# A new table of pieces for a four-layer graph network: where the projections and the feed-forward parts stand between the attention steps

## The chip, the cores and the metric

The kernel runs on one core of one Trainium2 chip. The metric is the device time of one launch in microseconds (us); less is better. Four engines share the work: PE (TensorE, the matrix unit, with its weight loads shown apart as PEld), DVE (VectorE), ACT (ScalarE) and POOL (GpSimd). SP (SyncE) issues the transfers.

## The reference

The input is `x`, 16 graphs of 1024 nodes with 128 features, and one 1024 x 1024 adjacency matrix `adj`. Three transformer layers and one graph attention layer follow each other. Cut to what matters:

```python
# layers 0, 1, 2 (8 heads of 16)
Q, K, V = (h @ Wq), (h @ Wk), (h @ Wv)               # split into heads
scores = einsum('bnhd,bmhd->bhnm', Q, K) / sqrt(16)
attn = softmax(where(adj == 0, -inf, scores))
x = layer_norm(h + (attn @ V) @ Wo + bo)
x = layer_norm(x + relu(x @ W1 + b1) @ W2 + b2)
# layer 3
h = x @ W
e = leaky_relu(h @ a_src [:, None] + h @ a_dst [None, :])
out = layer_norm(softmax(where(adj == 0, -inf, e)) @ h + x)
```

## The kernel before

**Blocks, halves and steps.** One graph in one of the layers 0 to 2 is a block; there are 48. Four graphs go through the three layers side by side, so the order is layer 0 of graphs 0 to 3, layer 1 of graphs 0 to 3, layer 2 of graphs 0 to 3, then the same for the next four graphs. A block has four halves: two groups of four heads (`g`) times two halves of the queries (`qh`). A half has eight steps, one for each 128 keys (`kt` 0 to 7). A block thus has 32 steps, and "step 12" below means the step at position 12 of its block.

**What a step issues.** `score_step` computes the scores of four heads for 128 keys and 512 queries: four matmuls (L423) into two PSUM tiles `s` of 1024 columns. For three of the eight `kt` (2, 5, 7, `BOTH_ON_DVE`) DVE adds the mask to both tiles (L433). For the others, ACT takes the exponential of the first tile straight from PSUM (L430) and POOL multiplies the mask in (L431), while DVE adds the mask to the second tile. Whatever DVE has masked gets its exponential on ACT afterwards (L445). Then `av_due` issues the attention product of the step four earlier (`AHEAD = 4`): matmuls (L450) into the accumulator `acc`. After the eighth product of a half, `finish` lets DVE transpose the accumulator into `tt` (L461), and only then may the first product of the next half write `acc`, since there is one such tile (`sums`). With a lag of four steps, the last product of a half is issued in steps 3, 11, 19 and 27, and the first product of the next half in steps 4, 12, 20 and 28.

**Buffers in PSUM.** There are three tiles `s` of two banks each, one bank `t` for all pieces (`bank()`), and the one accumulator. The scores of step n use two of the three tiles: the first needs the second tile of step n-2 to be read, the second needs the first tile of step n-1 to be read.

**Pieces.** Everything else is cut into pieces, and `piece()` issues at most one of them in a step, behind the product. A block's pieces are:

- `proj_tasks`, for the next block: `t0(0)`, `t0(1)` transpose the halves of `x` (L286, evicted by ACT); `split("Wk", h)` and `split("Wq", h)` project k and q (below K0, K1, Q0, Q1). ACT copies the bank into `hi` (L385), then DVE subtracts `hi` from the bank into `lo` (L386), and the bank is free only after both. `v(h)` projects v (ACT copies).
- `post_tasks`, for the block before: `both` (two DVE transposes L477, nothing on PE), `out_proj(h)` (op0, op1: DVE adds the residual, L329, and takes statistics, L322 and L324; then POOL normalises, L337 to L341), `x1t(h)` (transposes of the normalised rows, ACT evicts), `ffn1(f, h)` (f00, f10, f01, f11 by f and h; ACT applies the relu, L506), `ffn2(h)` (F20, F21: twice as many matmuls, and the same DVE and POOL work as `out_proj`).
- `last_tasks`, for the fourth layer of a graph that has left layer 2: two transposes, three pieces of node projections (`nodes`), `rows_gh` with 16 small DMAs, edges (L610 on DVE) and aggregations of 124 to 128 matmuls, and an end with POOL work and the output DMA.

**Order.** The engines PE and ACT keep the order in which this code issues; DVE, POOL and SP are ordered by the scheduler. The table `AT` gives each piece of `proj` and `post` the earliest step of its block; a chain's pieces stay in order. `last_tasks` have gaps instead of steps, stand in the same chain behind the `post` pieces of their block, and take any step whose piece isn't due. `piece()` asks the chains in order, `proj` first. By reading the queues, the pieces of a block without `last_tasks` fall like this (30 of the 48 blocks):

```
step    0   3    6    8   9  10   11 12  14 17 19 20 22  23   25   26  27  28  30
before  F20 t0.0 t0.1 F21 K0 both K1 op0 Q0 Q1 v0 v1 op1 x1t0 x1t1 f00 f10 f01 f11
```

In the 12 blocks with `last_tasks` throughout, almost every other step is taken too. `stack` (L408) brings `hi` and `lo` into the layout of the scores with 16 DMAs on SP; it is issued for the next block's first group at step 21, after its last projection.

Of the kernel before, what the change touches and what calls it, by code (L numbers as in the profile page):

```python
# [30 lines left out]
FIRST = 1  # L31


AT = {"proj": (3, 6, 9, 11, 14, 17, 19, 20), "post": (12, 22, 23, 25, 26, 27, 28, 30, 32, 40, 41)}
AT_END = {3: (12, 21, 22, 24, 25, 26, 27, 28, 30, 31), 2: (8, 9, 13, 14, 15, 16, 17, 18, 20, 21)}
AHEAD = 4
BOTH_ON_DVE = (2, 5, 7)
TILES = {"w": 10, "x": LANES + 1, "last": 2}
# [77 lines left out]
def fast_path(ctx: ExitStack, tc: tile.TileContext, a: dict, out: bass.AP, flag):  # L116
# [160 lines left out]
    def soon():  # L277

        return nullcontext() if head[0] else tc.high_priority(offset=SOON)
# [22 lines left out]
    def rows(v, n=NT):  # L302
        return v[:, None, :].to_broadcast([P, n, D])
# [53 lines left out]
    def proj_tasks(m):  # L357
        b, l = blocks[m]
        w = W[l]
        s = {}  # L360

        def t0(h):
            def run():
                x = state["x", b]
                if l == 0:
                    s["xT", h] = transpose_half("xT", x, h)
                    if h == 1:
                        nc.gpsimd.tensor_add(x, x, rows(w["bo"]))
                else:

                    s["xT", h] = transpose_half("xT", x, h, W[l - 1]["ln2_gc"], W[l - 1]["ln2_bc"])
                    if h == 1:
                        scale_shift(x, W[l - 1]["ln2_g"], w["bo"])
            return run

        def split(n, h):
            def run():
                if h == 0:
                    state[n, m] = [work.tile([P, N], F32R, tag="hl", name=i, bufs=4) for i in ("hi", "lo")]
                hi, lo = state[n, m]  # L380
                c = slice(h * 512, (h + 1) * 512)
                ps = bank()
                by_columns(ps, w[n], s["xT", h])
                with soon():
                    nc.scalar.copy(hi[:, c], ps)  # L385
                    nc.vector.tensor_sub(lo[:, c], ps, hi[:, c].bitcast(F32))  # L386
            return run

        def v(h):
            def out(ts, ps):  # L390
                with soon():
                    nc.scalar.copy(v_bufs[m % 2][:, ts].rearrange("p t h s -> p (t h) s")[:, :, :HD],
                                   ps.rearrange("p (m d) -> p m d", d=HD))
            return lambda: project([s["xT", h]], [w["Wv"]], h, out)

        pieces = [t0(0), t0(1), split("Wk", 0), split("Wk", 1), split("Wq", 0), split("Wq", 1), v(0), v(1)]
        return [(2 if n in (3, 4, 5, 6) else 1, f, {0: "+w", 1: "+w", 6: "-w", 7: "-w"}.get(n, "")) for n, f in enumerate(pieces)]

    behind = {}

# [68 lines left out]
    def post_tasks(b, l):  # L469
        w = W[l]  # L470
        s = {}
        att, recs = state["A"], state["recs"]

        def gather(h):
            def run():
                s["aT", h] = half_tile("aT")
                nc.vector.transpose(s["aT", h], att[:, h].rearrange("p k g d -> p (k g d)"))  # L477
                if h == 1:
                    check_range(recs.rearrange("p g h k -> p (g h k)"))
            return run  # L480

        def out_proj(h):
            def run():
                if h == 0:
                    s["n1"] = with_stats(state["x", b])
                project([s["aT", h]], [w["Wo"]], h, add_and_stats(s["n1"]))
                normalise(s["n1"], slice(4 * h, 4 * h + 4))
            return run

        def x1t(h, alone=False):  # L490
            def run():
                x1 = s["n1"][0]
                s["x1T", h] = transpose_half("x1T", x1, h, w["ln1_gc"], w["ln1_bc"])
                if alone:
                    scale_shift(x1[:, 4 * h:4 * h + 4, :], w["ln1_g"], w["b2"])
                elif h == 1:
                    scale_shift(x1, w["ln1_g"], w["b2"])
            return run

        def ffn1(f, h):  # L500
            def run():
                s["h", f, h] = half_tile("hT")
                ps = bank()
                by_columns(ps, w["W1"][:, f * P:(f + 1) * P], s["x1T", h])
                with soon():
                    nc.scalar.activation(s["h", f, h], ps, AF.Relu, bias=w["b1"][:, f:f + 1], scale=1.0)  # L506
            return run

        def ffn2(h):
            def run():  # L510
                if h == 0:
                    s["n2"] = with_stats(state["x", b])
                project([s["h", f, h] for f in range(NF)], [w["W2"][:, f, :] for f in range(NF)], h,
                        add_and_stats(s["n2"]))
                normalise(s["n2"], slice(4 * h, 4 * h + 4))
            return run

        def both():
            gather(0)()
            gather(1)()  # L520


        together = [(5, both, "+w +w"), (1, out_proj(0), "-w"), (1, out_proj(1), "-w"), (5, x1t(0), "+w"), (1, x1t(1), "+w")]
        for h in range(2):
            together += [(1, ffn1(0, h), "+w"), (1, ffn1(1, h), "+w -w")]
        together += [(1, ffn2(0), "-w -w"), (1, ffn2(1), "-w -w")]
        alone = [[(1, gather(h), "+w"), (1, out_proj(h), "-w"), (3, x1t(h, True), "+w"), (1, ffn1(0, h), "+w"),
                  (1, ffn1(1, h), "+w -w"), (1, ffn2(h), "-w -w")] for h in range(2)]
        return together, alone
# [161 lines left out]
    def piece():  # L691
        for chain in chains:
            if is_due(chain) and take(chain):
                return
# [27 lines left out]
    waiting = deque()  # L722
# [39 lines left out]
    n = 0  # L762
    with tc.manual_schedule(engines={mybir.EngineType.PE, mybir.EngineType.Activation}):
        for m, (b, l) in enumerate(blocks):
            order = [(g, qh) for g in range(G) for qh in range(2)]
            if m in (0, len(blocks) - 1):
                order.sort(key=lambda x: x[1])
            for at, (g, qh, kt) in enumerate((g, qh, kt) for g, qh in order for kt in range(NT)):
                now[0] = n
                if at == (6 if m == 0 else 1):  # L770
                    stack(m, 1)
                if n == 6:
                    with tc.issue_after(behind["stack"]):
                        first_weights()
                        other_weights()
                if n == 20:
                    with tc.issue_after(behind["pool"]):
                        biases()
                if n == 40:
                    with tc.issue_after(behind["dve"]):  # L780
                        last_weights()
                if at == 0 and m + 2 < len(blocks) and blocks[m + 2][1] == 0:
                    put([(0, fetch(blocks[m + 2][0]), "+x")], ("fetch", blocks[m + 2][0]))
                if m + 1 < len(blocks):
                    if at == (6 if m == 0 else 0):
                        need(("post",) + (blocks[m + 1][0], blocks[m + 1][1] - 1) if blocks[m + 1][1] else
                             ("fetch", blocks[m + 1][0]))
                        put(proj_tasks(m + 1), ("proj", m + 1), first=True)
                    if at == (24 if m == 0 else 21):
                        need(("proj", m + 1))  # L790
                        stack(m + 1, 0)
                step = m, g, qh, kt
                if FIRST <= n < FIRST + 4:

                    with tc.manual_schedule(engines={mybir.EngineType.DVE}):
                        e = score_step(step)
                        neighbours(4 + n - FIRST)
                        masks(4 + n - FIRST, mask_rows(4 + n - FIRST))
                else:
                    e = score_step(step)  # L800
                waiting.append((step, e, n + AHEAD))
                av_due(n)
                piece()
                n += 1
        exponentials(0)
        for n in range(n, n + 2 * AHEAD):
            now[0] = n
            av_due(n)
            piece()
        tail[0] = True  # L810
        while chains:
            now[0] += 1
            for chain in list(chains):
                if is_due(chain):
                    take(chain)
# [11 lines left out]
    both = const.tile([1, 2], F32)  # L827
# [224 lines left out]
```

## Time and profile before

| | |
|---|---|
| median of 3 runs | 3983.76 us (3979.37 to 3984.21) |
| the profiled execution | 3983.09 us, of which the span is 3981.2 us |
| granted TensorE clock | 0.987 |
| busy in the span | PE 3758.5, DVE 3408.3, ACT 3392.8, POOL 3331.4 us |
| a block without `last_tasks` (from 1440.72) | 73.14 us; busy PE 70.67, ACT 69.26, DVE 65.12, POOL 64.62 us |
| a block with them (from 931.92) | 97.01 us |

The time of a block is the distance between the first score matmuls of two blocks in the timeline of PE; a step's likewise. A matmul's end in the trace is modelled, and matmuls overlap, so the work of PE is read here from the distances between starts. PE counts as busy in nearly all of the span for that reason, whether or not it is at its peak.

### The profile page before, as it was taken

To read this page: it belongs to the slowest core of one execution; us is meant where nothing else is said; L and a number is where in the kernel's file an instruction comes from. 1 tells how busy PE (TensorE), PEld (TensorE's weight loads), DVE (VectorE), ACT (ScalarE), POOL (GpSimd) and SP (SyncE) were. 2 spreads that over 40 slices of the span, in tenths; PEclk is the share of its full clock that TensorE was granted. 3 is DMA by queue.
4 is the path that set the end of the run, shared out by engine and by line. 5 is a ranking of instruction groups with operands and counts; after the bars stand their busy time and mean duration, and the time that the engine had idled before them with its cause. 6 is when DMAs were issued, how large, how long until landed. Compare 5 with 4: busy or idle time off the path is not lost.

```text
span 3981.2 us, 107823 instructions
## 1 busy us (share of the span) xinstructions
PE 3758.5 (94%) x44501; PEld 1558.5 (39%) x44501; DVE 3408.3 (86%) x5326; ACT 3392.8 (85%) x3961; POOL 3331.4 (84%) x3010
## 2 busy tenths in 40 slices
PE   7999999999999999999999999999999999999996
PEld 2333333344443333334444333333444433333345
DVE  7888988988888988988888898888888898898874
ACT  7999999977779999997777999999777799999860
POOL 4788888987789888988778888888877898898875
PEclk8999999999999999999999999999999999999998
DMA  6222222112222222222222222221222212222200
GB/s 163 65 65 53 55 65 63 46 48 65 56 58 57 65 65 54 54 65 55 55 55 55 65 53 56 65 64 45 55 55 55 71 46 62 65 51 58 66 8 20
DMA packets 124465, 233.13 MB, mean 59 GB/s; under 512 B 34624, under 2 KB 73792, under 8 KB 123968
## 3 DMA queue, kind: packets, MB, share of 16 engines
q1 hardware_dynamic: 123056, 225.74, 22.5%
q8 instruction: 354, 5.80, 0.6%
q14 instruction: 143, 1.17, 0.1%
q10 hardware_dynamic: 912, 0.42, 0.0%
HBM read 15.54 MB, written 8.39 MB: 6 GB/s over the span
## 4 chain that ended last, share of the span: by engine, by line
PE 61%; DVE 22%; POOL 9%; ACT 4%; issue 3%; SPq 0%; DMA 0%; DVEq 0%; ACTq 0%; POOLq 0%
PE acc L450 23%; PE t L297 19%; PE s L423 16%; DVE e L433 13%; POOL e L431 3%; POOL x L341 2%; PE t L286 2%; DVE lo L386 2%; DVE st L322 2%; ACT e L445 2%; ACT e L430 2%; DVE tt L461 1%; POOL mv L339 1%; PE s L297 1%; POOL x L345 1%
## 5 line engine op out<-in xcount | busy, mean ns | idle before, releaser
L433 DVE TENSOR_TENSOR e<-s,mask_add 128x1024 f32<-128x1024 f32 x2112 | 2493.6, 1213 | 344.6 <-PE s L423 263.7
L445 ACT ACTIVATE e<-e 128x1024 f32<-128x1024 f32 x2112 | 2203.4, 1060 | 206.1 <-DVE e L433 187.9
L431 POOL TENSOR_TENSOR e<-e,mask 128x1024 f32<-128x1024 f32 x960 | 1933.5, 2026 | 419.0 <-ACT e L430 419.0
L450 PE MATMUL acc<-e,v 128*17 128x512 f32 x12288 | 1627.8, 601 | 73.3 <-DVE tt L461 47.8
L423 PE MATMUL s<-Wq,Wk 64*128 64x512 f32 x6144 | 1185.0, 456 | 58.1 <-DVE e L433 41.3
L430 ACT ACTIVATE e<-s 128x1024 f32<-128x1024 f32 x960 | 980.8, 1022 | 227.5 <-PE s L423 226.5
L423 PEld LDWEIGHTS s<-Wq,Wk 64*128 64x128 f32 x6144 | 501.2, 185 | 1027.9 <-DVE e L433 417.1
L450 PEld LDWEIGHTS acc<-e,v 128*17 128x17 f32 x12288 | 208.6, 95 | 582.1 <-issue 452.0
L341 POOL TENSOR_SCALAR x<-x,mv 128x128 f32<-128x128 f32 x896 | 389.1, 447 | 23.5
L345 POOL TENSOR_TENSOR x<-x,ln_g 128x1024 f32<-128x1024 f32 (+1 forms) x97 | 229.5, 2367 | 25.1 <-PE t L286 22.6
L339 POOL TENSOR_TENSOR mv<-mv,half_neg 128x4 f32<-128x4 f32 x224 | 232.4, 1038 | 18.6
L297 PE MATMUL t<-hd,e 128*32 128x129 f32 x7040 | 208.2, 275 | 1.2
L329 DVE TENSOR_TENSOR x<-t,x 128x512 f32<-128x512 f32 x191 | 130.8, 685 | 86.9 <-PE t L297 86.9
L297 PEld LDWEIGHTS t<-hd,e 128*32 128x32 f32 x7040 | 194.6, 110 | 16.0 <-issue 5.0
L322 DVE BATCH_NORM_STATS2 st<-x 128x6 f32<-128x128 f32 x896 | 197.3, 280 | 3.3
L297 PE MATMUL t<-x1T,W 128*32 128x512 f32 x1520 | 198.0, 592 | 0.0
L297 PEld LDWEIGHTS t<-W,hT 128*32 128x32 f32 x6080 | 170.0, 110 | 58.5 <-issue 45.5
L297 PE MATMUL t<-W,hT 128*32 128x128 f32 x6080 | 183.4, 273 | 0.2 <-DVE x L625 0.2
L286 PE MATMUL t<-identf,x 128*128 128x128 f32 x872 | 151.0, 289 | 34.0 <-DVE lo L386 15.4
L286 PEld LDWEIGHTS t<-identf,x 128*128 128x128 f32 x872 | 92.9, 141 | 230.2 <-issue 108.3
L337 POOL TENSOR_SCALAR mv<-mv 128x4 f32<-128x4 f32 x224 | 53.0, 236 | 124.6 <-DVE mv L324 98.8
L610 DVE SCALAR_TENSOR_TENSOR e<-s,mask 128x1024 f32<-128x1024 f32 x128 | 150.3, 1214 | 5.9 <-PE s L607 5.0
(118 smaller groups left out, 2573.9 us busy)
## 6 DMA issues: line engine op xcount, KB each, us to landing
Wk<-hi SPq DMA_DIRECT2D x384, 128.0 KB
Wk<-lo SPq DMA_DIRECT2D x384, 128.0 KB
Wq<-hi SPq DMA_DIRECT2D x384, 128.0 KB
Wq<-lo SPq DMA_DIRECT2D x384, 128.0 KB
x<-in_x_dram SPq DMA_DIRECT2D x16, 512.0 KB
out_dram<-x SPq DMA_DIRECT2D x31, 256.0 KB
ai<-in_adj_dram SPq DMA_DIRECT2D x8, 512.0 KB
g_rows<-parts SPq DMA_DIRECT2D x124, 4.0 KB
```

Of the source, the lines that this page charges most:

```text
L286: nc.tensor.transpose(ps[:, t * P:(t + 1) * P], src[:, 4 * h + t, :], identf)
L297: nc.tensor.matmul(dst[j:j + SLOT, :], lhsT[:, j:j + SLOT], rhs, start=start, stop=stop)
L322: nc.vector.bn_stats(st[:, t, :], z[:, t, :])
L339: nc.gpsimd.tensor_tensor(v, v, half_neg[:, ts], OP.pow)
L341: nc.gpsimd.tensor_scalar(z[:, t, :], z[:, t, :], mv[:, t, 0:1], mv[:, t, 1:2], op0=OP.add, op1=OP.mult)
L345: nc.gpsimd.tensor_mul(z, z, rows(gain, n))
L423: nc.tensor.matmul(ps[:, r * 512:(r + 1) * 512], k[64 * r:64 * r + 64, kt * P:(kt + 1) * P], q[64 * r:64 * r + 64, q0:q0 + 512], start=Tru ...
L430: nc.scalar.activation(ev, psv, AF.Exp, scale=HD ** -0.5)
L431: behind["pool"] = nc.gpsimd.tensor_mul(ev, ev, m).ins
L433: behind["dve"] = nc.vector.tensor_add(ev, psv, m).ins
L445: nc.scalar.activation(ev, ev, AF.Exp, scale=HD ** -0.5)
L450: nc.tensor.matmul(acc[j * SLOT:j * SLOT + HD + 1, :], v_bufs[m % 2][:, kt, 2 * j + g, :], e[:, j, :], start=first, stop=last)
```

## The change

Three things are altered. First, the step loop: if the product that is due opens a half, the piece goes ahead of the product, right behind the scores; in all other steps it stays behind the product. Second, the order of two chains: v0 and v1 stand between K0 and K1 now, and `x1t(1)` stands behind the two `ffn1` of the first half. Third, the table: where a piece may run.

```diff
-AT = {"proj": (3, 6, 9, 11, 14, 17, 19, 20), "post": (12, 22, 23, 25, 26, 27, 28, 30, 32, 40, 41)}
-AT_END = {3: (12, 21, 22, 24, 25, 26, 27, 28, 30, 31), 2: (8, 9, 13, 14, 15, 16, 17, 18, 20, 21)}
+AT = {"proj": (4, 6, 10, 12, 13, 16, 18, 20), "post": (14, 22, 24, 25, 26, 28, 29, 30, 32, 40)}
+AT_END = {3: (14, 19, 22, 23, 24, 25, 26, 27, 28, 30), 2: (8, 9, 13, 14, 15, 16, 17, 18, 20, 21)}
...
-        pieces = [t0(0), t0(1), split("Wk", 0), split("Wk", 1), split("Wq", 0), split("Wq", 1), v(0), v(1)]
-        return [(2 if n in (3, 4, 5, 6) else 1, f, {0: "+w", 1: "+w", 6: "-w", 7: "-w"}.get(n, "")) for n, f in enumerate(pieces)]
+        return [(1, t0(0), "+w"), (1, t0(1), "+w"), (1, split("Wk", 0), ""), (1, v(0), ""), (1, v(1), ""),
+                (1, split("Wk", 1), ""), (1, split("Wq", 0), "-w"), (1, split("Wq", 1), "-w")]
...
-        together = [(5, both, "+w +w"), (1, out_proj(0), "-w"), (1, out_proj(1), "-w"), (5, x1t(0), "+w"), (1, x1t(1), "+w")]
+        together = [(5, both, "+w +w"), (1, out_proj(0), "-w"), (1, out_proj(1), "-w")]
         for h in range(2):
-            together += [(1, ffn1(0, h), "+w"), (1, ffn1(1, h), "+w -w")]
+            together += [(1, x1t(h), "+w"), (1, ffn1(0, h), "+w"), (1, ffn1(1, h), "+w -w")]
...
-                    if at == (24 if m == 0 else 21):
+                    if at == (24 if m == 0 else 22):
...
                 waiting.append((step, e, n + AHEAD))
+                begins = waiting[0][2] <= n and waiting[0][0][3] == 0
+                if begins:
+                    piece()
                 av_due(n)
-                piece()
+                if not begins:
+                    piece()
                 n += 1
```

In a block without `last_tasks` the pieces then fall like this, with a bar where the piece stands ahead of the product:

```
step    0   4     6    8   9    10 12  13 14  16 18 20  22  24   25  26  28    29  30
after   F20 t0.0| t0.1 F21 both K0 v0| v1 op0 K1 Q0 Q1| op1 x1t0 f00 f10 x1t1| f01 f11
```

The number of pieces, of matmuls, of evictions and of DMAs is the same. `stack` for the next block is issued one step later.

## The prediction

> **What bounds the kernel.** I read the page's first section, then the windows of one ordinary block (no `last_tasks`) cut at the four products that open a half, then PE's and DVE's timelines around such a cut. The windows, in us: length, then busy time and count of PE, PEld, DVE, ACT, POOL, then clock and DMA.
>
> ```profile
> 1451.51:1469.46 17.95, 17.38 (x181) 6.56 (x181) 17.50 (x28) 17.72 (x21) 17.10 (x12) 1.00 0.04 9
> 1469.46:1487.61 18.15, 17.33 (x176) 6.13 (x177) 16.84 (x26) 16.82 (x20) 16.60 (x18) 1.00 0.28 71
> 1487.61:1506.21 18.60, 18.35 (x184) 6.82 (x184) 15.51 (x23) 17.72 (x21) 14.34 (x14) 1.00 0.17 45
> 1506.21:1524.65 18.44, 17.61 (x182) 6.42 (x181) 15.27 (x22) 16.99 (x20) 16.58 (x16) 1.00 0.46 114
> ```
>
> The clock is whole, and DMA is idle for the most part. PE leads, but ACT has 17.72 of 17.95 and 17.72 of 18.60, and DVE 17.50 of 17.95: whatever PE wins meets the next engine within 2%.
>
> A bare step takes PE 1.645 us (starts of scores in steps 1 to 2). A projection, a v, an `op` or an `ffn1` adds 0.87, a transposing piece 0.59, F20 or F21 1.75. An ordinary block is therefore worth 32 x 1.645 + 12 x 0.87 + 4 x 0.59 + 2 x 1.75 = 68.9; it takes 73.14. The 4.2 between are lost at five places: steps 3 and 4 (1.2), 12 (0.65), 14 to 17 (0.85), 20 (0.63), 24 and 25 (0.8). Step 12 looks like this on PE, and on DVE:
>
> ```profile
> 1466.31 1.05 PE L450 MATMUL acc<-e,v 128*17 128x512 f32 x8
> 1467.18 1.04 PE L297 MATMUL t<-xT,Wk 128*32 128x512 f32 x8
> 1468.15 0.73 PE L423 MATMUL s<-Wq,Wk 64*128 64x512 f32 x4
> 1469.46 1.05 PE L450 MATMUL acc<-e,v 128*17 128x512 f32 x8 [0.57 <-DVE tt L461]
> ```
>
> ```profile
> 1465.75 0.68 DVE L386 TENSOR_TENSOR lo<-t,hi 128x512 fp32r<-128x512 f32 x1
> 1466.35 2.35 DVE L433 TENSOR_TENSOR e<-s,mask_add 128x1024 f32<-128x1024 f32 x2
> 1468.61 0.70 DVE L461 STREAM_TRANSPOSE tt<-acc 128x512 f32<-128x512 f32 x1
> 1469.29 0.69 DVE L386 TENSOR_TENSOR lo<-t,hi 128x512 fp32r<-128x512 f32 x1
> ```
>
> The last product of the half ends at 1467.3, yet `tt` starts at 1468.61, because DVE still has two mask additions of 1.14 each in front of it. The wait is DVE's backlog, and the piece in between (K1) is already cover. Over the whole run:
>
> ```profile
> PE acc L450 <- DVE tt L461: 47.8, 84, 1.0
> PE s L423 <- DVE e L433: 41.3, 108, 0.9
> ```
>
> The loss of steps 14 to 17 is the second row: the scores wait for a tile `s` that DVE reads late.
>
> **What the Trainium skill says.** "PSUM — Partial Sum Buffer", Specifications (TRN2): eight banks a partition. Three `s` of two banks, `t` and the accumulator are all eight, so nothing here can be double-buffered instead of reordered. The same page, Engine vs sequencer instructions: the queues of ACT, DVE and POOL are strict FIFO, and matmuls start in program order. The trace agrees: the product above stands behind 0.57 of waiting with no later matmul passing it. "Perfetto Trace Analysis", Identifying the Most-Contended Engine: matmul busy time is no measure of distance from the limit. It agrees too: PE shows 70.67 busy where distances between starts give 68.9.
>
> **The change, part by part.** I carry the queues through an ordinary block by hand, with those PE pitches, DVE 1.14 an addition, 0.65 `tt` or `x`, 1.06 statistics, 0.6 `lo`, and ACT 0.9 for L430, 0.95 for L445, 0.5 to 0.7 for an eviction (starts of neighbours in the timelines). By these rules the stretch from step 12 of before gives scores at 10.0 into the stretch where the trace has 1479.48, also 10.02; so I trust the rules. Times are from the product that opens each half.
>
> *The piece ahead of the opening product.* Before, the order is last product, piece, scores, opening product; after, last product, scores, piece, opening product. Between the two products lies the same PE work, 0.66 + 0.87, so by itself this covers no more of `tt`. It gives DVE and ACT the scores 0.6 to 0.9 earlier, which helps only where they have nothing to do. I cost it at nothing; DVE's backlog hides it.
>
> *Steps 4 to 12.* t0(1), F21, K0 and one more piece, as before, but v0 for K1. DVE is full (17.50). K0 moves one step later, so its `lo` lands close to `tt`. If `lo` goes first, `tt` ends and v0 is through at 17.8; if `tt` goes first, v0 must wait for bank `t`, and the product opens at 18.5. Against 17.95: -0.15 or +0.55. I take +0.15.
>
> *Steps 12 to 20.* Before: op0, Q0, Q1, v0. After: v1, op0, K1, Q0, Q1, all one bare step apart but v1 and op0. Work on PE 13.16 + 5 x 0.87 = 17.5; ACT needs about 17, DVE 16.3. In my walk the waits are 0.3 (step 18, ACT frees the tile late), 0.2 (step 20) and 0.3 (`tt`): 18.2 to 18.5 with one piece more than the 18.15 of before. +0.2.
>
> *Steps 20 to 28.* Before v1, op1, x1t0, x1t1, f00, f10; after op1, x1t0, f00, f10, x1t1, one piece of 0.87 less. PE work 16.95, but ACT has 16 exponentials (14.9), one `hi`, one x1T and two relus: 17.2. ACT frees the last tile 0.4 late in step 28. 17.75 for 18.60: -0.85.
>
> *Steps 28 to 4.* The same pieces. F20's residual and statistics and four additions stand ahead of `tt` on DVE as before. 18.15 for 18.44: -0.3.
>
> Sum: -0.8 for an ordinary block, between -1.6 (the freer DVE order everywhere) and +0.2 (`lo` behind `tt`, ACT 0.2 worse in each half). Thirty such blocks: -24, from -48 to +6.
>
> *Blocks with `last_tasks`.* Here gaps, not the table, place the pieces, so the two promises don't hold. Reading the queues: a3 falls in step 11, n03 or n36 in step 19, x1t0 or rows in step 27, all right ahead of a piece that now follows after 0.66 of scores instead of 1.64 of scores and product; and xt1 or a3 follow K1, n03 or xt1 follow Q0. op0 slips from step 12 to 22 to 25, so that x1t0 comes three to four steps behind it, about 6 to 8 us, where the chain DVE to POOL has taken 6 to 9 (op1 to x1t1, steps 22 to 25 and 22 to 26). For a late bank the trace has this row (nodes in step 26, a transpose in step 27):
>
> ```profile
> 1018.83 0.66 PE L286 MATMUL t<-identf,x 128*128 128x128 f32 x4 [0.70 <-DVE hd L575]
> ```
>
> With 0.7 to 0.9 for such a pair, 0.3 to 0.7 more where the gap shrinks to 0.66, and 1.5 for x1t0, the first partly filled block of a group (77.4 us, four of them) loses 2.7. For the other twelve (93 to 99 us) losses and gains nearly cancel: they lose 6.8 to 10.7 already, at xt0 behind Q0 and xt1 behind Q1 (0.83 each), which the new order turns into fewer pairs. I take -0.5 each, from -2 to +3. Together 4 x 2.7 - 12 x 0.5 = +5, from -13 to +47.
>
> *Other edits.* `stack` a step later: 16 issues of 0.6 on SP are 10 us, and ten steps, over 20 us, remain until the next block; SP's later issues (`rows`, 16 more) have eight steps of gap before e0. Cost nothing; if that cover went, the first scores of a block would wait for `Wq<-lo`, as they do once now (5.0). x1t1 nearer to F20: POOL's scale and shift (2 x 2.39, behind two masks of 2.0) takes 8.4 and must be done before F20's residual, 11 later in ordinary blocks (nothing), 8.4 in full ones (0 to 1, inside the range). `AT_END[3]` concerns one block: nothing.
>
> Net: -24 + 5 = -19 on the profiled execution's 3983.1, which lies within 0.7 of the median, so 3964.
>
> **The rivals.** *Same:* `tt` is DVE-bound everywhere and ACT has no room, so what one stretch gains, the next gives back. For it speaks that work between the two products is unchanged and that ACT is at 99% in one stretch. Then ordinary blocks give -0.3 each, -9, and the full ones +5: 3979. *Slower:* the single bank `t` in full blocks. If a piece ahead of an opening product waits 0.7 for the one just before the scores, at three half-starts a block, and x1t0 waits 1.5 for op0's chain, that is 3.6 for each of 16 blocks, +58; the ordinary -24 makes +34, 4017. It decides from about 2 us a full block on, where it outweighs them. Against it: at step 12 and 20 the opening product waits for `tt` anyway, so part of it is hidden. *Nothing done:* excluded, since the code reorders PE and ACT itself. *Much faster:* DVE's scheduler puts `tt` ahead of the additions; then the waits of steps 4, 12 and 20 go, 1.2 more in a block, 36 in all: 3928.
>
> **Numbers.** A measurement can tell about 0.2%, 8 us. My forecast has 0.45, much faster 0.12, same 0.17, slower 0.26. The forecast's own range is 3940 to 3982; with the upper rivals the range is 3930 to 4010, leaving out the deepest gains and the worst of the full blocks. Some of the forecast (0.03) ends above 3976 and so within 8 us of before, and some of the same case (0.03) beyond it; so faster 0.55, same 0.16, slower 0.29.
>
> **What would show it.** Right: ordinary blocks of 72.3 in place of 73.1, with the stretch from step 20 the most shortened and the loss of steps 14 to 17 gone; PE's wait for `tt` still some 40 us in all; ACT's idle for DVE smaller; first partly filled blocks over 79. Wrong: the wait for `tt` near zero (then the move ahead of the product covers more than I say), ordinary blocks over 73, or full blocks longer by over 3.

## The result: slower by 1.1%

The changed kernel takes 4026.78 us (median of 4 runs, 4024.36 to 4027.93) against 3981.86 us before (median of 4, 3979.37 to 3984.21). The ratio is 1.0112, with a 95% interval from 1.0095 to 1.013. The prediction said 3964, between 3930 and 4010; it missed the direction and the range.

The profiled execution took 4024.36 us with a span of 4022.5, against 3983.09 and 3981.2. The clock is 0.986 (0.987 before), so the clock is no part of the difference. By the starts of the first score matmuls of all blocks, the 41.3 us between the two spans lie here:

| where | before | after | difference | predicted |
|---|---|---|---|---|
| 30 ordinary blocks | 2193.1 | 2211.6 | +18.5 | -24 |
| 16 blocks that hold `last_tasks` | 1469.6 | 1488.5 | +18.9 | +5 |
| first and last block, start and end of the kernel | | | +3.9 | 0 |

An ordinary block took 73.15 us and takes 73.79. These are medians of the 30, and so are the times of ordinary blocks in all runs below; times of full blocks are sums over the 16 that hold `last_tasks`. Those are numbered 10 to 14 below: blocks 10 and 11 of each twelve and the first three of the next. The windows of one ordinary block, cut at the products that open a half (length, then busy time and count of PE, PEld, DVE, ACT, POOL, then clock and DMA), stand against the four shown of before:

```profile
1467.39:1485.53 18.14, 17.57 (x205) 7.16 (x208) 17.45 (x28) 17.44 (x20) 17.20 (x13) 1.00 0.04 11
1485.53:1504.02 18.49, 18.07 (x193) 6.31 (x186) 16.28 (x25) 17.46 (x21) 16.46 (x17) 1.00 0.18 44
1504.02:1522.66 18.64, 17.84 (x156) 5.79 (x148) 15.87 (x24) 17.07 (x21) 13.29 (x14) 1.00 0.28 71
1522.66:1541.19 18.53, 17.80 (x182) 6.31 (x182) 15.29 (x23) 17.13 (x20) 17.64 (x16) 1.00 0.46 112
```

All four stretches are longer than before: by 0.19, 0.34, 0.04 and 0.09. The third has one piece of 0.87 less than it had, and is no shorter. PE shows the most busy time everywhere. The other engines have no more work than before: the sums of busy time of DVE, ACT and POOL in this block are each within 0.3 of those of before.

What PE waited for over the whole run is told by these rows of the waits (total us, times, longest), with the row of DVE's that will matter:

```profile
DVE lo L386 <- ACT hi L385: 56.9, 69, 2.5
PE s L423 <- DVE e L433: 42.4, 81, 0.9
PE s L423 <- ACT e L430: 40.4, 125, 1.2
PE acc L450 <- DVE tt L461: 4.2, 8, 1.0
```

The wait for `tt` (47.8 before) is all but gone: 4.2. In its place stands the wait of the scores for ACT: 40.4, where it was 0.7 before. The wait of the scores for DVE has not moved (41.3 before). So **the wait has changed its place, and little of it has gone**. These rows do not hold the 41 us, though: with the same matmuls PE counts as busy for 3798.5 us, 40.0 more than before, since the ends of matmuls are modelled. They say where PE waits; what a step loses is read from distances between starts.

The place is step 12. PE's timeline, from the last product of the half (1482.15) to the first of the next (1485.53), ACT's, and DVE's `tt`:

```profile
1482.15 1.05 PE L450 MATMUL acc<-e,v 128*17 128x512 f32 x8
1483.14 0.50 PE L423 MATMUL s<-Wq,Wk 64*128 64x512 f32 x2
1484.21 0.49 PE L423 MATMUL s<-Wq,Wk 64*128 64x512 f32 x2 [0.57 <-ACT e L430]
1484.63 1.08 PE L297 MATMUL t<-Wv,xT 128*32 128x128 f32 x32
1485.53 1.04 PE L450 MATMUL acc<-e,v 128*17 128x512 f32 x8
```

```profile
1480.51 2.25 ACT L445 ACTIVATE e<-e 128x1024 f32<-128x1024 f32 x2 [0.57 <-DVE e L433]
1482.67 0.57 ACT L385 CAST hi<-t 128x512 fp32r<-128x512 f32 x1
1483.13 1.03 ACT L430 ACTIVATE e<-s 128x1024 f32<-128x1024 f32 x1
```

```profile
1484.38 0.70 DVE L461 STREAM_TRANSPOSE tt<-acc 128x512 f32<-128x512 f32 x1
```

Before, the product opened this half after 0.57 of waiting for `tt`. Now it opens without a wait, but the scores ahead of it have waited the same 0.57. Their second tile must first be read by ACT's exponential of the step before, and that starts at 1483.13, behind K0's `hi`. Before, K1 stood ahead of these scores and gave ACT 0.87 for it. And `tt` is made no sooner: it starts 2.23 after the start of the last product, where it was 2.30 before (1466.31 to 1468.61 in the prediction's lines). The product finds it ready because the scores ahead of it have waited.

Step 22 is the largest new loss. DVE's timeline (`lo` there is Q1's), ACT's and PE's:

```profile
1504.74 0.23 DVE L463 RECIPROCAL recs<-tt 128x16 f32<-128x16 f32 x1
1505.72 0.69 DVE L386 TENSOR_TENSOR lo<-t,hi 128x512 fp32r<-128x512 f32 x1 [0.75 <-ACT hi L385]
1506.33 3.48 DVE L433 TENSOR_TENSOR e<-s,mask_add 128x1024 f32<-128x1024 f32 x3
```

```profile
1503.22 1.04 ACT L430 ACTIVATE e<-s 128x1024 f32<-128x1024 f32 x1
1504.13 1.08 ACT L445 ACTIVATE e<-e 128x1024 f32<-128x1024 f32 x1
1505.07 0.61 ACT L385 CAST hi<-t 128x512 fp32r<-128x512 f32 x1
```

```profile
1506.63 0.49 PE L423 MATMUL s<-Wq,Wk 64*128 64x512 f32 x2
1507.60 0.50 PE L423 MATMUL s<-Wq,Wk 64*128 64x512 f32 x2 [0.47 <-DVE e L433]
```

Q1 stands on PE from 1503.14, but ACT has two exponentials in front of `hi`. DVE's queue has put `lo` ahead of three additions. DVE stands still for 0.75, then does `lo`, and begins the additions at 1506.33. PE started the scores of the first of them at 1504.99 and takes 0.5 for such a tile, so by this estimate they begin 0.8 late. The scores of step 22 then wait for a tile that DVE has not read yet. The Trainium skill, "PSUM — Partial Sum Buffer", Engine vs sequencer instructions, calls the queues of VectorE and ScalarE strict FIFO (what is queued first runs first); the trace agrees: PE has written scores of step 21 from 1504.99 on, and no addition passes the waiting `lo`. In the whole run DVE waits 56.9 us for `hi` now (the row above); before it was 0.9.

Step by step, with the pitches of the prediction (1.645 for a bare step and the price of its piece taken off the distance between scores), an ordinary block loses this, in us:

| step | 3 | 4 | 12 | 14 to 18 | 20 | 22 | 24, 25 | 28 | sum |
|---|---|---|---|---|---|---|---|---|---|
| before | 0.86 | 0.31 | 0.65 | 0.86 | 0.63 | 0 | 0.80 | 0 | 4.1 |
| after | 0.85 | 0.41 | 0.86 | 0.63 | 0.35 | 0.74 | 0.55 | 0.44 | 4.8 |

Step 20 gains 0.28, and steps 14 to 18 and steps 24 and 25 about 0.25 each. Steps 4, 12, 22 and 28 take more than that back, most of it in 22 and 28.

### The profile page after: what moved, and what is told of

It reads as the page before. It is cut to its first block, busy times and chain, and to the rows that moved or that the text cites. A ratio compares the mean times of both kernels' runs of the same rounds, so it can differ in the third digit from the quotient of the medians.

```text
span 4022.5 us, 107873 instructions
## 1 busy us (share of the span) xinstructions
PE 3798.5 (94%) x44501; PEld 1548.1 (38%) x44501; DVE 3393.6 (84%) x5326; ACT 3375.8 (84%) x3961; POOL 3330.5 (83%) x3010
## 5 line engine op out<-in xcount | busy, mean ns | idle before, releaser
L423 PE MATMUL s<-Wq,Wk 64*128 64x512 f32 x6144 | 1209.6, 458 | 97.2 <-DVE e L433 42.4
L297 PE MATMUL t<-hd,e 128*32 128x129 f32 x7040 | 208.9, 276 | 5.1 <-DVE lo L386 5.1
L329 DVE TENSOR_TENSOR x<-t,x 128x512 f32<-128x512 f32 x191 | 130.6, 684 | 96.3 <-PE t L297 95.7
L297 PE MATMUL t<-x1T,W 128*32 128x512 f32 x1520 | 199.6, 597 | 6.2 <-ACT x1T L291 1.8
L297 PEld LDWEIGHTS t<-hd,e 128*32 128x32 f32 x7040 | 194.2, 110 | 21.3 <-issue 7.8
L297 PEld LDWEIGHTS t<-W,hT 128*32 128x32 f32 x6080 | 175.5, 112 | 59.5 <-issue 46.7
L297 PE MATMUL t<-W,hT 128*32 128x128 f32 x6080 | 189.2, 278 | 0.2 <-DVE x L625 0.2
L386 DVE TENSOR_TENSOR lo<-t,hi 128x512 fp32r<-128x512 f32 x188 | 128.6, 684 | 51.7 <-ACT hi L385 51.7
```

Of the source, the lines that this page charges most:

```text
L297: nc.tensor.matmul(dst[j:j + SLOT, :], lhsT[:, j:j + SLOT], rhs, start=start, stop=stop)
L423: nc.tensor.matmul(ps[:, r * 512:(r + 1) * 512], k[64 * r:64 * r + 64, kt * P:(kt + 1) * P], q[64 * r:64 * r + 64, q0:q0 + 512], start=Tru ...
```

## The experiments

Every time below is a median, and every ratio is to the kernel before on the same chip, with its 95% interval; the changed kernel stands at 1.0112. The block times come from the profile of each run.

### The parts alone

**The new table without the placing.** All pieces stand behind the product again:

```diff
-                begins = waiting[0][2] <= n and waiting[0][0][3] == 0
-                if begins:
-                    piece()
                 av_due(n)
-                if not begins:
-                    piece()
+                piece()
```

> The changed kernel with every piece behind the product, in opening steps too. Nothing but 0.66 of scores then stands between the last product of a half and the next opening one. Theory A: tt needs up to 1.8 after the last product, so each of 192 openings waits 0.5 to 0.9 more than it does in the changed kernel, less the waits of the scores that end: 4050 to 4130. Theory B (placing does not matter): 4020 to 4035.

Measured: 4071.79 us, 1.0223 (1.0206 to 1.024), as the first theory had it; ordinary blocks 75.22. PE's wait for `tt` is back, and larger than before the change (47.8):

```profile
PE acc L450 <- DVE tt L461: 63.8, 88, 1.6
```

So with the new table the placing is worth 45 us, where I had costed it at nothing. At steps 20 to 22 it is worth nothing, though: 1.06 here, 1.09 in the changed kernel.

**The placing without the new table.** This is the kernel before with the `begins` edit alone.

> The kernel before with one edit: the piece of an opening step goes ahead of the product. Table and chains are the old ones, so op0, v1 and f01 move ahead of the openings of steps 12, 20 and 28, with K1, v0 and f10 still in the step in front. Theory A (the wait changes its place, it does not go): tt's waits (47.8 in all) nearly vanish, but the moved piece now waits for bank t, or the scores for a tile, by about as much: ordinary block 73.0 to 73.8, 3980 to 4010. Theory B (cover for tt is worth what the wait was): ordinary block 72.0, about 3945.

Measured: 4040.91 us, 1.0147 (1.013 to 1.0164); ordinary blocks 74.22. The placing alone costs 58 us, more than the first theory had, and the second missed the direction. PE at step 12, then DVE:

```profile
1486.10 1.05 PE L450 MATMUL acc<-e,v 128*17 128x512 f32 x8
1486.97 1.04 PE L297 MATMUL t<-xT,Wk 128*32 128x512 f32 x8
1487.94 0.73 PE L423 MATMUL s<-Wq,Wk 64*128 64x512 f32 x4
1489.82 1.08 PE L297 MATMUL t<-Wo,aT 128*32 128x128 f32 x32 [1.15 <-DVE lo L386]
```

```profile
1488.39 0.70 DVE L461 STREAM_TRANSPOSE tt<-acc 128x512 f32<-128x512 f32 x1
1489.07 0.69 DVE L386 TENSOR_TENSOR lo<-t,hi 128x512 fp32r<-128x512 f32 x1
```

K1 still fills bank `t` in step 11, and op0, now ahead of the product, wants it after nothing but scores. It waits 1.15 for a `lo` that stands behind `tt`. In the whole run PE waits 0.8 us for `tt` now, and 52.3 for `lo` at pieces of L297, where it was 3.5: the wait for `tt` has become one for the bank. Alone the table and the placing cost 88 and 58 us, together 45.

**The piece ahead of the scores as well.** In the steps that open a half, `piece()` is called before `score_step`.

```diff
+                begins = len(waiting) > 0 and waiting[0][2] <= n and waiting[0][0][3] == 0
+                if begins:
+                    piece()
                 ...score_step...
-                begins = waiting[0][2] <= n and waiting[0][0][3] == 0
-                if begins:
-                    piece()
```

> The changed kernel, but in a step that opens a half the piece goes ahead of the scores too (last product, piece, scores, opening product), which is the order that the kernel before has. Theory A (the wait has moved: with the scores right behind the last product, their second tile waits for ACT to read the step before, and the piece's eviction stands behind two more exponentials on ACT): the waits of the opening product for tt come back (over 30 us in all), the waits of the scores shrink, and the net lies between the two kernels, 3985 to 4015. Theory B (the loss sits in the order of the two chains, not in this placing): 4020 to 4035.

Measured: 4084.76 us, 1.0253 (1.0236 to 1.027); ordinary blocks 74.85, full ones +44.9 against before. Both expectations missed. This order gives ACT the time back that step 12 lacks, and the scores' waits for ACT fall to 7.8. PE waits only 3.7 for `tt`, not over 30. But v0 now stands right behind the last product of the half, with only a step without a piece between K0 and it, and the bank is still full:

```profile
1505.74 1.05 PE L450 MATMUL acc<-e,v 128*17 128x512 f32 x8
1508.18 1.08 PE L297 MATMUL t<-Wv,xT 128*32 128x128 f32 x32 [1.39 <-DVE lo L386]
1509.19 0.73 PE L423 MATMUL s<-Wq,Wk 64*128 64x512 f32 x4
```

```profile
PE t L297 <- DVE lo L386: 89.4, 81, 1.5
```

The Trainium skill, "Perfetto Trace Analysis", Matmuls, wants independent groups to rotate through PSUM banks, so that one is emptied while the next is computed. The runs show the price of a single one here: up to 1.5 us each time, 89.4 in all. There are thus three places for the piece, and each has its own wait. Behind the opening product, PE is left waiting for `tt`; between scores and product, for the scores' tile `s` with the new table and for bank `t` with the old one; ahead of the scores with the new table, for bank `t`.

**The new chain after attention alone** (op0 to F21 with the new order and steps; projections and placing as before).

> The kernel before with the new order and the new steps of the post chain alone (x1t1 behind the first two ffn1; op0 at 14 and so on), projections and placing as before. Theory A: op0 falls in step 15 behind Q0, x1t0 is followed at once by f00, which waits 0.35 for ACT; the ordinary block gains or loses under 0.5 and blocks with the fourth layer lose 1 to 2: 3980 to 4020. Theory B (the loss is in the order of the post chain): 4010 to 4035, nearly all of the 43.

Measured: 4000.03 us, 1.004 (1.0026 to 1.0055); ordinary blocks 73.68, the 16 full ones 1467.7. The total is in the range of the first theory. It costs 17 us, all of it in ordinary blocks. There op0, due from step 14, falls in step 15 behind Q0 and loses 1.08, of which the trace shows 0.86 as waiting for bank `t`; but step 16 no longer loses its 0.59, so steps 14 to 18 are 0.3 worse together. Step 28, where x1t1 stands now, loses 0.53 that it did not lose before, and steps 24 and 25 win 0.26. The full blocks are even 2 faster, so this chain alone is not what hurts them.

**The old chain after attention, in the changed kernel.**

> The changed kernel with the old order and the old steps of the post chain; new projections and the piece ahead of the opening product stay. Theory A: the late eviction of K0 and Q1 on ACT stays (0.8 in step 12, 0.7 in step 22), so most of the loss stays: 4000 to 4030. Theory B (the loss is in the order of the post chain): back to 3975 to 3995.

Measured: 4099.14 us, 1.0289 (1.0271 to 1.0306); ordinary blocks 74.11, but the 16 full ones 1561.5. Both expectations missed. In full blocks op0 slips to steps 22 to 25 by the new order of projections, and x1t0 and x1t1 follow at once. In blocks 10 to 13 x1t1 then waits 3.6, 6.0, 2.5 and 1.5 us for the rows that POOL normalises, in steps 26, 28, 29 and 30. In the changed kernel, with x1t1 behind two `ffn1`, the longest such wait is 0.5.

### Single causes in the changed kernel

**Q1's `hi` copied by DVE**, which then need not wait for ACT there:

```diff
-                    nc.scalar.copy(hi[:, c], ps)
+                    if n == "Wq" and h == 1:
+                        nc.vector.tensor_copy(hi[:, c], ps)
+                    else:
+                        nc.scalar.copy(hi[:, c], ps)
```

> The changed kernel with hi of Q1 alone copied by DVE instead of ACT. Theory A (step 22 loses 0.74 because DVE's queue stands still at lo of Q1 until ACT, behind two exponentials, has written hi): DVE no longer stands still, at the price of 0.6 of DVE work; step 22 loses under 0.4, ordinary block 73.2 to 73.6, 4005 to 4020. Theory C (DVE is late there for its own work, not for ACT): step 22 loses 0.7 to 1.3, 4025 to 4050.

Measured: 4011.62 us, 1.0074 (1.0057 to 1.0091); ordinary blocks 73.53. It is 15 us faster than the changed kernel, although DVE got 0.6 more work a block (behind Q1, which stands in step 20). In the profiles 7.5 of it lie in the 30 ordinary blocks and 4.2 in the full ones. The total is as expected; step 22 fell from 0.74 to 0.47, not quite below 0.4. DVE and the row of waits:

```profile
1500.84 0.68 DVE L386 CAST hi<-t 128x512 fp32r<-128x512 f32 x1
1501.44 0.23 DVE L466 RECIPROCAL recs<-tt 128x16 f32<-128x16 f32 x1
1501.59 0.65 DVE L389 TENSOR_TENSOR lo<-t,hi 128x512 fp32r<-128x512 f32 x1
1502.16 2.35 DVE L436 TENSOR_TENSOR e<-s,mask_add 128x1024 f32<-128x1024 f32 x2
```

```profile
DVE lo L389 <- ACT hi L388: 22.0, 23, 2.4
```

There is no gap between the four. The edit also spares ACT a copy, but ACT then stands still for 1.07 from 1502.4 on, waiting for DVE, so that is not what helped here. Of the 0.74 of step 22, 0.27 are thus shown to come from the stall of DVE's queue; 0.47 stay, with `hi` and `lo` still ahead of the additions. All in all this edit takes back a third of the 45 us.

**K0 at step 9 in place of 10**, so that its `hi` is out of ACT's way at step 12.

> The changed kernel with K0 back in step 9 (the two transposes of both go to step 10). Theory A (step 12 loses 0.86 because hi of K0 stands on ACT ahead of the exponential of step 11 that frees the tile for the scores of step 12): loss of step 12 under 0.5, ordinary block 73.3 to 73.5, 4008 to 4020. Theory C (DVE's load before tt decides): step 12 stays at 0.7 to 0.9, 4020 to 4032.

Measured: 4037.67 us, 1.014 (1.0123 to 1.0157). The row in question falls from 40.4 to this:

```profile
PE s L423 <- ACT e L430: 17.1, 86, 0.3
```

The wait for ACT has more than halved, but steps 11 and 12 still lose 0.65 for 0.86, as much as in the kernel before, and the scores' wait for DVE rises from 42.4 to 53.5. So `hi` in front of the exponential explains 0.2 of the loss; behind it stands DVE, which fits the second theory. Ordinary blocks win that 0.2 (73.59). The full blocks lose 15.6 (1504.1), and the total goes the wrong way, out of both ranges: one entry of the table also moves 16 blocks that it was not meant for.

**v1 last** (K0 v0 K1 Q0 Q1 v1 from steps 9, 12, 14, 16, 18, 20; op0 from 13), so that the piece of step 20 needs no `hi` and `lo`.

> The changed kernel with K0 in step 9, v1 at the end of the projections (step 20, ahead of the opening product), K1, Q0, Q1 in steps 14, 16, 18 and op0 in 13. v1 needs one copy on ACT and nothing of DVE. Theory A: steps 20 and 22 together lose under 0.5 in place of 1.1, ordinary block 72.6 to 73.3, whole 3985 to 4010 since blocks with the fourth layer stay as they are. Theory C (openings are bound by DVE's load anyway): ordinary block 73.5 or more, 4015 to 4035.

Measured: 4014.88 us, 1.0081 (1.0064 to 1.0098); ordinary blocks 72.93, now below those of before, but the full ones 1506.6. Step 22 loses 0.01 instead of 0.74: it is the eviction of Q1 in step 20, by two engines, that step 22 paid for. But step 20 now loses 0.81 instead of 0.35, so the expectation of less than 0.5 for both missed. The total missed too, since the full blocks lost 18.

**x1t0 at step 23**, one bare step ahead of f00 instead of right before it.

> The changed kernel with x1t0 in step 23 instead of 24, so that one step lies between x1t0 and f00. Theory A (f00 loses 0.35 in step 25 because ACT has not yet evicted the transposes of step 24): steps 24 and 25 together lose under 0.2 in place of 0.55, step 28 keeps its 0.44, ordinary block 73.3 to 73.5, whole 4012 to 4020. Theory F (ACT's queue is late there whatever stands before it, and the loss turns up a step or two later): ordinary block 73.7 or more, 4023 to 4032.

Measured: 4012.2 us, 1.0068 (1.0052 to 1.0083); ordinary blocks 73.56. The total is as expected, the reason not: steps 24 and 25 keep 0.63, while step 28 falls from 0.44 to 0.12. So part of what step 28 lost was handed on from x1t0's step; that ACT's backlog handed it on was not tested. What steps 24 and 25 lose stays open.

### Ordinary and full blocks apart

In the next five kernels the tables, the order of the chains and the placing are chosen by block: full means the 16 blocks that hold `last_tasks`, and all others count as ordinary. Where no order is given it is that of before.

```diff
-AT = {"proj": (...), "post": (...)}
+AT = {"proj": (full, ordinary), "post": (full, ordinary)}
...
-                begins = waiting[0][2] <= n and waiting[0][0][3] == 0
+                begins = (full, ordinary)[plain()] and waiting[0][2] <= n and waiting[0][0][3] == 0
```

**The whole change in full blocks only.**

> The kernel before, with the whole change (order, table, placing) only in blocks 10 to 14 of each twelve, those that run the fourth layer; ordinary blocks stay as before. Theory A (two separate losses, 0.65 in each ordinary block and about 7 in each five blocks with the fourth layer): 20 to 26 above before, 4003 to 4010. Theory D (those blocks lose only because the ordinary ones around them come out differently): within 8 of before.

Measured: 3997.67 us, 1.0042 (1.0028 to 1.0056), which is 16 us, between the two expectations; ordinary blocks 73.14 as before. About a third of the 45 us of the change is thus made in full blocks alone.

**v1 last, in ordinary blocks only.**

> Ordinary blocks with the order K0, v0, K1, Q0, Q1, v1 (steps 9, 12, 14, 16, 18, 20), op0 in 13, the new post chain and the piece ahead of the opening product; blocks with the fourth layer as before. Theory A: ordinary blocks keep 72.9 and the others theirs, 30 x -0.2: 3974 to 3982. Theory D: the gain is lost again, 3990 or more.

Measured: 3977.91 us, 0.9993 (0.9984 to 1.0001); ordinary blocks 72.93. That is as the first theory had it, and no difference that can be told.

**An evenly spread table, all pieces behind the product, in ordinary blocks only.**

> Ordinary blocks with the order K0, v0, K1, Q0, Q1, v1 in steps 9, 11, 14, 16, 18, 20, everything behind the product, old post chain (op0 in 12); other blocks as before. Theory A (a projection followed at two steps' distance loses nothing between openings, and the placing ahead of the product is not needed): the 0.85 of steps 14 to 17 shrinks to under 0.4, but at step 20 nothing except scores covers tt, 1.0 for 0.63; ordinary block 72.9 to 73.4, 3975 to 3992. Theory E (the placing ahead of the product is what made 72.9): 73.5 or more, 3993 or more.

Measured: 4010.99 us, 1.0076 (1.0062 to 1.009); ordinary blocks 74.02. The even spread alone is no gain: steps 14 to 18 lose 0.69, and step 20 1.69 where it was 0.63. The wait for `tt` is the price, as in the first experiment:

```profile
PE acc L452 <- DVE tt L463: 65.4, 84, 1.2
```

**The same on odd steps**, with nothing in step 12 or 20, x1t1 at 26 and the `ffn1` from 27 to 30.

> Ordinary blocks with K0, v0, K1, Q0, Q1, v1 in steps 9, 11, 13, 15, 17, 19, op0 in 12, everything behind the product, x1t1 in 26 and the four ffn1 in 27 to 30; other blocks as before. Theory A: v1 in step 19 covers tt as v0 did, the steps 13 to 18 lose under 0.5 in place of 0.85, and x1t1 a step later no longer waits 0.5 for POOL: ordinary block 72.3 to 73.0, 3958 to 3980. Theory C (DVE's load, not the order, sets these losses): 73.1 or more, 3983 or more.

Measured: 3979.97 us, 0.9997 (0.9988 to 1.0005); ordinary blocks 72.98, at the edge of what was expected, and again no difference. Steps 13 to 18 lose 0.73, not under 0.5, and of the 0.5 that step 25 lost, 0.28 stay there and 0.2 have moved to step 26.

**The placing at two of the four opening products.** K0 v0 K1 Q0 Q1 v1 from steps 9, 12, 14, 16, 18, 20, the piece ahead of the product in steps 12 and 20 only, the chain after attention as before (op0 from 13), in ordinary blocks only:

```diff
+                begins = plain() and at in (12, 20) and waiting[0][2] <= n and waiting[0][0][3] == 0
```

> Ordinary blocks put together from the best stretch of each run so far: K0, v0, K1, Q0, Q1, v1 in 9, 12, 14, 16, 18, 20 with the piece ahead of the product at steps 12 and 20 alone, t0(0) behind the product in step 3, the old post chain from step 22; op0 in 13; blocks with the fourth layer as before. Theory A (losses of a stretch add up): 72.9 less 0.1 (steps 3 and 4) less 0.2 (steps 24 to 28) is 72.6, whole 3964 to 3974. Theory F (what one stretch gains the next gives back): ordinary block 72.9 to 73.2, 3976 to 3986.

Measured: 3971.22 us, **0.9968 (0.9956 to 0.998)**, against 3984.46 for the kernel before on the same chip; ordinary blocks 72.72. The total is in the range of the first theory. This version beats both kernels. Its timeline at step 12, three rows of PE's waits and one of DVE's:

```profile
1464.57 1.05 PE L452 MATMUL acc<-e,v 128*17 128x512 f32 x8
1465.86 0.78 PE L425 MATMUL s<-Wq,Wk 64*128 64x512 f32 x4 [0.24 <-DVE e L435]
1466.57 1.08 PE L297 MATMUL t<-Wv,xT 128*32 128x128 f32 x32
1467.71 1.05 PE L452 MATMUL acc<-e,v 128*17 128x512 f32 x8
```

```profile
PE s L425 <- DVE e L435: 42.0, 110, 0.9
PE acc L452 <- DVE tt L463: 13.5, 25, 1.0
PE s L425 <- ACT e L432: 7.1, 35, 0.5
DVE lo L386 <- ACT hi L385: 39.0, 66, 2.3
```

K0 is three steps away, and the scores wait 0.24 for DVE, not 0.57 for ACT. By the rows, much of PE's waiting has gone: 13.5 for `tt` and 7.1 for ACT, with the one for DVE as before. By the distances between starts, though, steps 11 and 12 still lose 0.67, as in the kernel before (0.68), and step 20 0.82 for 0.63. The gain lies in steps 14 to 18, 0.26 for 0.86, where K1, Q0 and Q1 stand two steps apart. With nearly the same table and everything behind the product, two runs above, these steps lost 0.69 and step 20 1.69, so the spread alone does not do it. DVE still waits 39.0 us for `hi` here, so that wait is not by itself what a block loses.

### Why the full blocks lose

No run was made for a single step of them; this is read from the trace of the changed kernel. To its own 18 pieces with work on PE a full block adds up to 11 of the fourth layer. In block 13, 28 of the 32 steps have work for PE, and a table cannot keep the step behind a projection empty. PE there:

```profile
1096.57 1.05 PE L450 MATMUL acc<-e,v 128*17 128x512 f32 x8
1098.75 3.75 PE L297 MATMUL t<-hd,e 128*32 128x129 f32 x128 [1.13 <-DVE lo L386]
...
1103.97 1.04 PE L297 MATMUL t<-xT,Wq 128*32 128x512 f32 x8
...
1105.70 1.05 PE L450 MATMUL acc<-e,v 128*17 128x512 f32 x8
1108.22 0.63 PE L286 MATMUL t<-identf,x 128*128 128x128 f32 x4 [1.47 <-DVE lo L386]
```

An aggregation behind K1 waits 1.13 for the bank, a transpose behind Q0 1.47. Before, in this block, two pieces of transposes stood behind Q0 and Q1 and waited 0.8 each; the first of them:

```profile
1083.69 0.63 PE L286 MATMUL t<-identf,x 128*128 128x128 f32 x4 [0.79 <-DVE lo L386]
```

At openings (steps 12, 20 and 28) a piece ahead of the product waits for the bank too, in each of the five kinds of full block, 0.4 to 1.1 each time. From block 10 to 14 the means went from 77.8 to 79.2, 96.1 to 97.0, 97.6 to 96.3, 98.9 to 101.6 and 93.3 to 95.6. Which of these pairs brings how much was not taken apart, so the cause in full blocks is read, not shown by a run.

## Why the prediction was wrong

**Steps 4 to 12 (+0.15 predicted, +0.19 measured)** and **12 to 20 (+0.2, +0.34)** came out near the sum, the first by luck. The walk had feared for v0's bank; the trace shows `lo` of K0 ahead of `tt`, the case for which the walk had -0.15, and no wait of v0 for the bank. In its place the scores waited 0.57 for ACT. In the second, 0.8 of waits were walked and 1.0 came: steps 14 to 18 0.63 for 0.3, step 20 0.35 for 0.2, and none of the 0.3 for `tt`.

**Steps 20 to 28 (-0.85, +0.04): the failed step.** The lack of one piece was right, and so was step 28 (0.4 said, 0.44 measured). The sum allows 0.8 for waits over the 16.95 of PE's work and names only the 0.4 of step 28; the other 0.4 has no term. Measured are 1.7: step 22 (0.74) and steps 24 and 25 (0.55) were left out. For step 22 the error is that I gave each engine its work in the stretch, 17.2 for ACT, and let `hi` and `lo` run when their data came. ACT's queue has two exponentials ahead of Q1's `hi`, DVE's queue stands still with it, and the additions come behind. With v1 in Q1's place step 22 loses nothing, and with `hi` on DVE 0.47. Why steps 24 and 25 lose is not known; they lost 0.80 before, and I had them at nothing.

**Steps 28 to 4 (-0.3, +0.09).** Step 3 loses 0.85 as before (0.86), step 4 0.41 for 0.31. I had the gain from nothing but a smoother walk; no step in it got one.

**"The piece ahead of the opening product: nothing."** This was the second failed step. The argument, equal PE work between the two products, was right: at step 12 `tt` starts 2.23 after the last product, for 2.30. What was put at nothing is the other side. The piece that stood ahead of the scores was also cover for their wait for tile `s`; I had the earlier scores only as something that may help. The wait for `tt` fell from 47.8 to 4.2, which the prediction had named as a sign that it was wrong. The meaning that it gave to this sign, that the move covers more of `tt`, was wrong too: at step 12 the wait stands ahead of the product now, and 40.4 came up at the scores. Without the new table the move costs 58 us, with it it saves 45.

**Full blocks (+5 predicted, +19 measured).** The slower rival had a mechanism that the trace shows, a late bank `t` at openings, at 0.4 to 1.1 for the 0.7 said, and a price of 3.6 a block; the net of all that changed is 1.2 a block on average. The first partly filled block was +2.7 and is +1.8 in three of four and +0.1 in the last. The other twelve were to win 0.5 each and lose 1.1: the term "fewer pairs" failed, since the pairs became different ones, and the two in block 13 wait 1.1 and 1.5 where it was 0.8.

**Other edits (0 predicted, +3.9 measured).** The last block, for which `AT_END` was called nothing, is 2.0 longer, and the very first scores come 1.8 later, after an opening in which v0 and v1 now stand between K0 and K1; neither was taken apart. Two small sums of the prediction are off, without weight here: POOL's scale and shift come to 8.8 by its own terms, not 8.4, and the chances to 0.54, 0.17 and 0.29. `stack` a step later brought no wait that the traces show: the scores' one wait for `Wq<-lo` is 3.9 us, where it was 5.0.

In all, ordinary blocks missed by 42.5 us, full ones by 14 and the rest by 4. The rival "same" had said that what one stretch gains the next gives back; that is what the ordinary blocks did, and somewhat more. The chance for slower, 0.29, was given to a mechanism in 16 blocks, while nearly half of the loss came from the 30 others, where I had put none.

## What to carry to other kernels

Work that is moved out of one gap was cover for everything behind it, not only for the wait that the profile names; list what each instruction behind the gap waits for before calling a move free. A row of waits that shrinks is no gain by itself; check the distances between starts. Where two in-order engines empty one bank in turn, walk the order of both queues, since the second engine can stand still with work ready. A table that fits one kind of block need not fit another, so try it on each kind alone: here the best version places a piece ahead of two of four products, in ordinary blocks only, and is 0.3% faster than the kernel before.

## What the runs showed of the hardware

The edits do not add up: 88 and 58 us alone became 45 together, and moving one entry of a table by one step (K0 from 10 to 9) won 0.2 us in each ordinary block and lost 15.6 us in the 16 others. And DVE took over a copy of 0.6 us a block from ACT, in a stretch where it was busy 15.87 of 18.64 and had stood still for 0.75, and the kernel became 15 us faster. A queue at a standstill is not always a loss, though: in the fastest version DVE waits 39.0 us for `hi`, in the changed kernel 56.9, in the kernel before 0.9.
